# A three-phase attention and mixture-of-experts kernel: storage shared between the phases, the second phase's first group prepared in the tail of the first, and another order inside its steps

## The chip, the cores and the metric

The kernel runs on one core of one Trainium2 chip. The metric is the device time of one execution in microseconds (us). The kernel before took 5142.19 us, the median of three runs (5132.47 to 5145.69). One further execution was taken by the hardware profiler; all rows below are from that one.

## The reference

The input is x, 8 x 1024 tokens of 256 numbers, in float32. Three things are computed in turn.

**Phase A**, an attention over channels. For each token, 16 heads of 64 channels; within a head, each channel of q looks at the channels of k up to its own:

```python
Q = (x @ Wq + bq).reshape(b, s, H, C) * inv_sqrt_c
scores = jnp.einsum('bshq,bshk->bshqk', Q, K)        # C x C per token and head, causal mask
attn = jnp.einsum('bshqk,bshk->bshq', softmax(scores), V)
x = layernorm(x + attn.reshape(b, s, HID) @ Wo + bo)
```

**Phase B**, an attention over the first axis (8 rows) with 4 heads of 64, apart for each of the 1024 positions, with a residual and a norm:

```python
o = attention_over_rows(x @ in_proj_w.T + in_proj_b)   # L = 8, N = 1024
y1 = ln(x + o @ out_proj_w.T + out_proj_b) * ln1_g + ln1_b
```

**Phase C**, a mixture of 8 experts. A softmax of `y1 @ wg` picks one expert for each token; each expert takes at most 1024 tokens in order; an expert is two matrices with nothing between them (256 to 1024 to 256, with biases). The result times the gate is added to y1 and normed, x is added, and a last norm gives the output.

## The kernel before

PE (TensorE) multiplies, ACT (ScalarE) does exponentials and copies, DVE (VectorE) does everything elementwise, POOL (GpSimd) a few elementwise operations and the issuing of many small transfers; SP only issues transfers. Every engine takes its instructions in the order in which the program emits them, since all three phases stand in a manual schedule. Transfers of SP and ACT share eight completion slots each in turn, so an issue also waits for the transfer that had its slot before.

**Phase A** (`phase_a`) goes over 64 tiles of 128 tokens, t = 0 to 63, and one more turn of the loop, t = 64, for the tail. A tile has 8 steps c. In a step, `scores` is called three times (which = 2, 0, 1): it spreads k over block-diagonal operands L and q over R, and PE fills pairs of PSUM banks (`pair`, three of them); ACT takes the exponential `e`. `sums` multiplies `e` with the spread values V into one PSUM bank, `S` is DVE's copy of it (L395), and POOL moves S into `nd` by transfers. `divide` (L414) makes `att`, `turn` transposes it, `output` multiplies with Wo (L445), `normal` (L456) makes x1, and `store` writes x1 to DRAM (L418). R and L are filled by transfers in `build`, two buffers each: R on POOL's queue, L on SP's with 16 issues for each of the four rounds of a tile. `gather` sets an event on POOL (L316) after a round's transfers, and PE waits for that event. The tables `between`, `after`, `fill_a` and `fill_b` say which piece of the tile before or after is emitted in which step.

When phase A ends its pools are released. What phase B needs is then allocated in their place: weights, biases and constants are loaded or built, ahead of phase B's work.

**Phase B** (`phase_b`) goes over 8 groups j of 128 positions times 8 rows; group j takes tiles j, j + 8, ..., j + 56 of phase A. `load_x` reads them back from DRAM, `turn_x` transposes them (L662), `project_qk` (L677) and `project_v` (L695) project. A group has four steps n, one for each pair of heads and half of the positions. In a step, `scores` (L715, L726) fills `sc`, DVE takes the maximum mx (L735), ACT the eight exponentials s (L744), and `normed` divides by the sums (L754, L755). One step later `turn_s` transposes s into the same PSUM banks (L760), ACT copies that to sT (L762), and `weighted` multiplies with the values (L772); ACT copies it to oT (L780). `fills` lists for each group the other pieces, four lists: projections of the next group (`nxt`), `residual`, `output` (L802), `normal` (L816, L819), `exps` and `choice` of the group before (`prv`), and pieces of experts 0 and 1. `some(k)` emits the next k pieces of the list; what is left follows at the step's end. `fill` PSUM banks are three. The group j = -1 only prepares group 0: it calls `center` and `beside`, which fold the norm's gain into the router's weights, and projects group 0.

The order inside a step is this, in `phase_b`:

```python
st = scores(j, c, ib)
some(1)
weights(st, 0)
sT = turn_s(before[3])      # the step before
some(2 if live else 0)
weights(st, 1)
normed(st)
weighted(*before[:3], sT)
some(len(work))
```

**Phase C** (`phase_c`) ranks the tokens with small matrix products, builds one-hot matrices (L1032, L1183, L1185, L1195) to find each slot's token, then gathers the rows with POOL (L1218) and multiplies with each expert's product of matrices. `load` fetches experts 2, 3 and 4 when the phase starts (L1044), and `expert` multiplies the two matrices (L1063); ACT copies the product (L1072).

Of the kernel before, what the change touches and what calls it, by code (L numbers as in the profile page):

```python
# [24 lines left out]
FP = mybir.dt.float32  # L25
# [18 lines left out]
CAP = L * N // E  # L44
RW = 2 * D + 1
# [5 lines left out]
def fused_kernel(ctx: ExitStack, tc: tile.TileContext, a: dict, out: bass.AP):  # L51
# [28 lines left out]
    phase_a(tc, a, ident, x1_d, norm_scalars)  # L80
# [12 lines left out]
    phase_b(tc, a, ident, x1_d, rows_d, lg_d, keep, norm_scalars)  # L93
    phase_c(tc, a, ident, rows_d, keep, out)
# [27 lines left out]
def phase_a(tc, a, ident, x1_d, norm_scalars):  # L122
# [11 lines left out]
    with (  # L134
# [19 lines left out]
        for n in ("k", "q", "v"):  # L154
            w[n] = wp.tile([P, DC, HID], FP, name=f"w{n}")
            nc.sync.dma_start(w[n], a[f"W{n}"].rearrange("(c p) f -> p c f", p=P))
        for n in ("k", "q"):
            bias[n] = wp.tile([P, HID], FP, name=f"b{n}")
            nc.scalar.dma_start(bias[n], a[f"b{n}"].partition_broadcast(P))
# [38 lines left out]
        for i in range(2):  # L198
            Ls.append(wp.tile([P, 16, 4, 32], FP, name=f"L{i}"))
            R = wp.tile([P, 4, 8, C1], FP, name=f"R{i}")  # L200
            nc.gpsimd.memset(R, 0.0)
            Rs.append(R)
            V = wp.tile([P, 2, H1, 4, 32], FP, name=f"V{i}")
            nc.gpsimd.memset(V, 0.0)
            for aa in range(4):
                nc.gpsimd.memset(V[32 * aa : 32 * aa + 32, :, :, :, 8 * aa + 4 : 8 * aa + 5], 1.0)
            Vs.append(V)
# [252 lines left out]


# [47 lines left out]
        for t in range(NT + 1):  # L509
            live, more = t < NT, t + 1 < NT  # L510
            for c in range(8):
# [15 lines left out]
                for job in fill_a.get(c, ()):  # L527
                    side(t, job)
                if live:
                    scores(t, c, 0)  # L530
# [9 lines left out]
        store(NT - 1)  # L540


def phase_b(tc, a, ident, x1_d, rows_d, lg_d, keep, norm_scalars):
# [8 lines left out]
    with (  # L552
        tc.tile_pool(name="bw", bufs=1) as wp,
        tc.tile_pool(name="bgroup", bufs=2) as gp,
        tc.tile_pool(name="bx", bufs=3) as xp,
# [6 lines left out]
        wi = wp.tile([P, DC, 3 * D + E], FP, name="wi")  # L562
        nc.scalar.dma_start(wi[:, :, : 3 * D], a["in_wT"].rearrange("(c p) f -> p c f", p=P))
        bqk = wp.tile([P, 4], FP, name="bqk")
        nc.scalar.dma_start(bqk, a["in_b_qk"].rearrange("(c p) -> p c", p=P))
        nc.vector.tensor_scalar(bqk[:, 0:2], bqk[:, 0:2], HW**-0.5, None, ALU.mult)
        rows = {}
        for n in ("in_b_v", "out_b", "ln1_g", "ln1_b", "ln2_b"):
            rows[n] = wp.tile([P, D + E], FP, name=f"row_{n}")
            nc.scalar.dma_start(rows[n][:, :D], a[n].partition_broadcast(P))  # L570

# [4 lines left out]
        cols = {}  # L578
        for n in ("ln1_g", "ln1_b", "out_b"):
            cols[n] = wp.tile([P, DC], FP, name=f"col_{n}")  # L580
            nc.scalar.dma_start(cols[n], a[n].rearrange("(c p) -> p c", p=P), allow_slow_non_contiguous=True)
        wg = wp.tile([P, DC, E], FP, name="wg")
        nc.sync.dma_start(wg, a["wg"].rearrange("(c p) e -> p c e", p=P))
# [7 lines left out]

        rep = wp.tile([P, L, B], BF, name="rep")
        other = wp.tile([P, L, B], BF, name="other")
        nc.vector.memset(rep, 0.0)
        nc.vector.memset(other, 0.0)
        for h in range(2):
            r = slice(h * HW, h * HW + B)
            nc.vector.tensor_copy(rep[r], ident[r, None, r].to_broadcast([B, L, B]))
            nc.vector.tensor_scalar(other[r], rep[r], -1.0, MASKED, ALU.add, ALU.mult)

        G = {}
# [4 lines left out]

        ww = wp.tile([P, DC, 3, E], FP, name="ww")
        wrow = wp.tile([P, 2, E], FP, name="wrow")

        def column(n):  # L610
            return cols[n][:, :, None].to_broadcast([P, DC, E])

        def center():
            w = ww[:, :, 0, :]
            nc.vector.tensor_tensor(w, wg, column("ln1_g"), ALU.mult)
            ps = pf.tile([P, 512], FP, name="fill")
            for c in range(DC):
                nc.tensor.matmul(ps[:, :E], keep["ones"], w[:, c, :], start=c == 0, stop=c == DC - 1)
            mean = wp.tile([P, E], FP, name="mean")
            nc.vector.tensor_scalar(mean, ps[:, :E], 1.0 / D, None, ALU.mult)  # L620
            nc.vector.tensor_tensor(w, w, mean[:, None, :].to_broadcast([P, DC, E]), ALU.subtract)
            nc.vector.tensor_copy(wi[:, :, 3 * D :], w)
            nc.vector.tensor_tensor(ww[:, :, 1, :], w, column("out_b"), ALU.mult)
            nc.vector.tensor_tensor(ww[:, :, 2, :], wg, column("ln1_b"), ALU.mult)

        def beside():
# [10 lines left out]
            sums = ps[:, DC * E : (DC + 2) * E]  # L637
            for c in range(DC):
                nc.tensor.matmul(
                    sums,  # L640
                    keep["ones"],
                    ww[:, c, 1:, :].rearrange("p k e -> p (k e)"),
                    start=c == 0,
                    stop=c == DC - 1,
                )
            nc.vector.tensor_copy(wout[:, :, D:], ps[:, : DC * E].rearrange("p (k e) -> p k e", k=DC))
            nc.vector.tensor_copy(wrow, sums.rearrange("p (k e) -> p k e", k=2))
            nc.vector.tensor_copy(rows["in_b_v"][:, D:], wrow[:, 0, :])

        def load_x(j):  # L650
            G["x", j] = xp.tile([P, L, D], FP, name="x")
            nc.sync.dma_start(G["x", j], x1_v[j])

        def turn_x(j, l0):
            if l0 == 0:
                G["xT", j] = wp.tile([P, DC, NB, L, B], FP, name="xT")
                G["qk", j] = gp.tile([P, DC, 2, N], FP, name="qk")
# [30 lines left out]
        def project_v(j, b):  # L688

            xT = G["xT", j].rearrange("p c b l n -> p c b (l n)")  # L690
            if b == 0:
                G["v", j] = gp.tile([P, NB, D + E], FP, name="v")
# [6 lines left out]
            if b == NB - 1:  # L699

                for l in range(L):
                    nc.sync.dma_start(
                        lg_d[j].rearrange("(b n) l e -> l n b e", n=B)[l],
                        G["v", j][l * B : (l + 1) * B, :, D:],
                    )
                lg = xp.tile([P, L, E], FP, name="lg")
                nc.sync.dma_start(lg, lg_d[j])
                G["lg", j] = lg
# [190 lines left out]
        def fills(j):  # L899
# [13 lines left out]
            put(0, j < 0, center)  # L913
# [4 lines left out]
            put(0, j < 0, beside)  # L918
# [47 lines left out]
        for j in range(-1, NJ + 1):  # L966
            if j < 0:
                load_x(0)
                load_x(1)
            parts = fills(j)  # L970
            for n in range(4):
# [9 lines left out]
                live = 0 <= j < NJ  # L981
                if live:
# [5 lines left out]
                    st = scores(j, c, ib)  # L988
                    some(1)
                    weights(st, 0)  # L990
                if before:
                    sT = turn_s(before[3])
                    some(2 if live else 0)
                if live:
                    weights(st, 1)
                    normed(st)
                if before:
                    weighted(*before[:3], sT)
                before = None
# [7 lines left out]
def phase_c(tc, a, ident, rows_d, keep, out):  # L1007
# [6 lines left out]
    with (  # L1014
# [4 lines left out]
        tc.tile_pool(name="cexp", bufs=3) as xp,  # L1019
# [14 lines left out]
        ex = {}  # L1034
# [3 lines left out]
        def load(e, halves=(0, 1), behind=None):  # L1038
            if 0 in halves:
                ex[e] = [xp.tile([P, FC, D], FP, name=n) for n in ("w1", "w2")]  # L1040
# [41 lines left out]

        for e in range(EARLY, EARLY + 3):
            load(e)
# [343 lines left out]
```

## Time and profile before

| what | value |
| --- | --- |
| median of three runs | 5142.19 us |
| the profiled execution, its own time | 5148.31 us |
| its span, from the first to the last instruction | 5146.6 us |
| ACT busy | 3349.6 us, 65% |
| POOL busy | 3292.1 us, 64% |
| first scores of phase B (L715), group 0 | 4385.08 us |
| first scores of groups 1 to 7 | 4431.95, 4488.43, 4545.69, 4603.06, 4661.01, 4719.00, 4774.92 us |
| last group's tail (group index 8) begins | 4832.60 us |
| phase C's first product (L1088) | 4859.74 us |

The profile page lists the busy time of each engine over the span, the span in 40 slices, the transfer queues, the chain of work that ended last, and groups of instructions by line. In the rows that follow, a line such as L772 is a line of the kernel, `fill<-sT,v` is output and inputs by name, and a bracket holds how long the engine stood idle before and what released it. A busy engine isn't always the one that sets the end: what matters is what the others wait for in that stretch. So the profile is read by stretches.

### The profile page before, as it was taken

The page shows a single profiled execution, that of the slowest core. Times are in us where ns is not written, and L with a number is a line of the kernel's source. Part 1 is how long each engine was busy: PE and PEld are TensorE (multiplying, and loading weights), DVE is VectorE, ACT ScalarE, POOL GpSimd, SP SyncE. Part 2 cuts the span into 40 slices and gives each one's busy share as a digit, 9 for nine tenths or more (in the row PEclk, how much of TensorE's full clock was granted, in tenths as well). Part 3 has the DMA queues.
Part 4 walks back from the last instruction along what each step waited for, and adds up shares of the span by engine and source line. Part 5 has one row for each costly group of instructions (what it writes and reads, how often), then busy time and mean ns, then how long its engine had stood idle before and what let it go on. Part 6 is the DMA issues. An engine that isn't in the chain of part 4 may idle for free.

```text
span 5146.6 us, 189171 instructions
## 1 busy us (share of the span) xinstructions
PE 4878.0 (95%) x79320; PEld 3271.6 (64%) x79320; DVE 3118.9 (61%) x6241; ACT 3349.6 (65%) x4123; POOL 3292.1 (64%) x6950
## 2 busy tenths in 40 slices
PE   7999999999999999999999999999999997888674
PEld 4666666666666666666666666666666664555452
DVE  5666565666666666566566666666656563577756
ACT  4777777777777777777777777777777774444233
POOL 5767677677677676766766766776776774133245
PEclk9999999999999999999999999999999998999797
DMA  2222222222222222222222222222222222222442
GB/s 75 47 48 48 48 49 46 48 48 48 46 48 49 46 48 49 47 48 48 47 47 48 49 46 48 49 46 48 49 48 48 49 48 60 53 74 74 119 150 91
DMA packets 586955, 287.05 MB, mean 56 GB/s; under 512 B 406257, under 2 KB 537713, under 8 KB 586097
## 3 DMA queue, kind: packets, MB, share of 16 engines
q1 hardware_dynamic: 376802, 112.30, 11.1%
q0 software_dynamic: 204800, 159.82, 10.5%
q8 instruction: 620, 10.16, 0.9%
q10 hardware_dynamic: 4496, 2.83, 0.2%
q14 instruction: 237, 1.94, 0.1%
HBM read 72.84 MB, written 33.85 MB: 21 GB/s over the span
## 4 chain that ended last, share of the span: by engine, by line
PE 87%; DVE 6%; ACT 3%; DMA 2%; issue 1%; another core or an unknown queue 1%; POOL 0%; SPq 0%; ACTq 0%; DVEq 0%; POOLq 0%
PE pair L345 26%; PE sum L375 20%; PE sum L384 9%; PE pair L333 8%; PE ps L236 5%; PE ps L268 5%; PE ps L225 5%; PE ps L445 5%; PE ps L427 1%; PE fill L677 1%; ACT s L744 1%; DVE mx L735 1%; DMA w<-in_w 1%; PE fill L772 1%
## 5 line engine op out<-in xcount | busy, mean ns | idle before, releaser
L361 ACT ACTIVATE e<-pair 128x1024 f32<-128x1024 f32 x3072 | 2977.2, 1021 | 1237.9 <-PE pair L345 1237.9
L405 POOL DMA_DIRECT2D nd<-S x4096 | 1949.0, 484 | 608.3 <-DVE S L395 415.9
L345 PE MATMUL pair<-R,L 32*128 32x128 f32 (+1 forms) x32768 | 1606.5, 323 | 3.4 <-POOL event L316 3.4
L395 DVE COPY S<-sum 128x512 f32<-128x512 f32 x1024 | 707.1, 691 | 1468.1 <-PE sum L384 1147.0
L345 PEld LDWEIGHTS pair<-R,L 32*128 32x128 f32 x32768 | 1271.7, 186 | 49.8 <-POOL event L316 4.3
L375 PE MATMUL sum<-e,V 128*32 128x256 f32 x16384 | 1284.9, 385 | 4.9 <-DVE S L395 4.9
L302 POOL DMA_DIRECT2D R<-qm x2048 | 973.9, 483 | 74.4 <-issue 39.3
L384 PE MATMUL sum<-e,V 128*32 128x128 f32 x16384 | 823.3, 273 | 0.0
L384 PEld LDWEIGHTS sum<-e,V 128*32 128x32 f32 x16384 | 532.9, 110 | 352.2 <-issue 0.9
L375 PEld LDWEIGHTS sum<-e,V 128*32 128x32 f32 x16384 | 406.3, 109 | 236.6 <-DVE vT L243 41.8
L333 PE MATMUL pair<-late,sel 32*128 32x256 bf16 (+1 forms) x6144 | 499.3, 313 | 9.6 <-ACT e L361 9.6
L256 DVE COPY V<-vT 32x128 f32<-32x128 f32 x2048 | 457.2, 223 | 28.1
L414 DVE RECIPROCAL att<-nd 128x256 f32<-128x256 f32 x256 | 447.4, 1748 | 7.8 <-DMA nd<-S 3.9
L333 PEld LDWEIGHTS <-sel 32*128 32x128 bf16 x6144 | 155.4, 91 | 460.4 <-issue 445.0
L316 POOL MEMSET event<- 1x1 f32 x256 | 22.6, 88 | 622.2 <-DMA R<-qm 422.1
L225 PE MATMUL ps<-wk,xT 128*128 128x512 f32 x512 | 257.9, 627 | 10.9 <-DMA wk<-in_Wk 10.1
L236 PEld LDWEIGHTS ps<-xT,wv 128*128 128x128 f32 x2048 | 238.2, 191 | 44.4 <-issue 41.8
L236 PE MATMUL ps<-xT,wv 128*128 128x128 f32 x2048 | 262.6, 281 | 1.6 <-DVE qm L269 0.8
L268 PE MATMUL ps<-wq,xT 128*128 128x512 f32 x512 | 255.7, 622 | 6.4 <-DVE k L226 6.4
L74 POOL TENSOR_SCALAR ve<-mv 128x1 f32<-128x1 f32 x128 | 33.7, 263 | 356.4 <-DVE mv L72 354.2
L445 PE MATMUL ps<-wo,attT 128*128 128x256 f32 x1024 | 257.9, 395 | 0.7 <-ACT attT L428 0.7
L445 PEld LDWEIGHTS ps<-wo,attT 128*128 128x128 f32 x1024 | 186.1, 191 | 63.7 <-issue 41.8
(203 smaller groups left out, 3762.2 us busy)
## 6 DMA issues: line engine op xcount, KB each, us to landing
R<-qm POOLq DMA_DIRECT2D x2048, 32.0 KB
nd<-S POOLq DMA_DIRECT2D x4096, 16.0 KB
L<-k SPq DMA_DIRECT2D x4088, 8.0 KB
rows_d<-yx SPq DMA_DIRECT2D x32, 512.0 KB
xT<-in_xT SPq DMA_DIRECT2D x64, 128.0 KB
xr<-in_x SPq DMA_DIRECT2D x64, 128.0 KB
x_d<-x1o SPq DMA_DIRECT2D x64, 128.0 KB
x<-x_d SPq DMA_DIRECT2D x8, 1024.0 KB
```

The costliest lines, as they stand in the source:

```text
L225: nc.tensor.matmul(ps, xT_of[t][:, c, :], w["k"][:, c, cols], start=c == 0, stop=c == DC - 1)
L236: nc.tensor.matmul(ps[:, i * P : (i + 1) * P], w["v"][:, c, ch * P : (ch + 1) * P], xT_of[t][:, c, :], start=c == 0, stop=c == DC - 1,)
L268: nc.tensor.matmul(ps, xT_of[t][:, c, :], w["q"][:, c, cols], start=c == 0, stop=c == DC - 1)
L302: moved.append((None, nc.gpsimd.dma_start(R[:, b, s, b, :], q[:, b, s, cols])))
L333: nc.tensor.matmul(bank[u].rearrange("p (n i) -> p n i", i=n)[:, :, 0:32], sel[pr].rearrange("p a j -> p (a j)"), late[pr, None, :].to_bro ...
L345: one = nc.tensor.matmul(bank[u][:, x * 4 * n : (x + 1) * 4 * n].rearrange("p (b i) -> p b i", i=n), Lt[pr, 2 * (h0 + h) + jb].rearrange(" ...
L361: nc.scalar.activation(e, pair[i], AF.Exp)
L375: nc.tensor.matmul(dst[32 * u : 32 * u + 32], Vs[ww][:, 0, h0 + h, u, :], e0[u // 2][:, u % 2, x * 256 : (x + 1) * 256].rearrange("p (b i) ...
L384: nc.tensor.matmul(dst[32 * u : 32 * u + 32, :, 32:], Vs[ww][:, 1, h0 + h, u, :], e1[u // 2][:, u % 2, h * 128 : (h + 1) * 128].rearrange( ...
L395: nc.vector.tensor_copy(S[:, :, 2 * which : 2 * which + 2, :].rearrange("p b h i -> p h b i"), ps.rearrange("p (h b i) -> p h b i", h=2, b=4),
L405: nc.gpsimd.dma_start(tok[:, b, s, h0 * C1 : (h0 + G) * C1], Sx[:, 4 if s else b, b, :])
L445: nc.tensor.matmul(ps[:, :D], attT[:, c, :], wo[:, c, :], start=c == 0, stop=c == HID // P - 1)
```

## The change

The kernel's pool `both`, which lives through all phases, now holds the weights, biases, one R and one V of phase A, and small tiles of phase B. `view` gives names to parts of them for later: phase B's weights wi, its x, xT, qk and v buffers, and the storage of phase C's experts.

```diff
+    view = {
+        "wi": share["wk"][:, :, : 3 * D + E],
+        "x": [ share["wq"]..., share["R"]... ],
+        "xT": share["wv"]...,
+        "qk": share["V"]...,
+        "v": share["bias"]...,
+    }
+    view["experts"] = [
+        [matrix(share["wk"], "c f"), matrix(share["wq"], "c f")],
+        [matrix(share["wv"], "c f"), matrix(share["bias"], "k f")[:, :FC, :]],
+        [V[:, :FC, :], V[:, FC:, :]],
+    ]
```

The preparation of group 0, which was the group j = -1 of phase B, becomes functions of phase A with a table of when each is called, by tile and step; (NT, 8) comes after the last store.

```diff
+        lead = {
+            (NT - 1, 1): [(lead_load, 0)],
+            (NT - 1, 3): [(lead_load, 1), (lead_mask,)],
+            (NT - 1, 5): [(lead_logits,)],
+            (NT - 1, 6): [(lead_load, 2)],
+            (NT, 0): [(lead_turn, 0), (lead_turn, 1)],
+            (NT, 1): [(lead_qk, 0, 0)],
+            (NT, 2): [(lead_qk, 0, 1)],
+            (NT, 8): [
+                (lead_v, 0), (lead_v, 1), (lead_qk, 1, 0),
+                (lead_qk, 1, 1), (lead_v, 2), (lead_v, 3),
+            ],
+        }
...
                 for job in fill_a.get(c, ()):
                     side(t, job)
+                for fn, *args in lead.get((t, c), ()):
+                    fn(*args)
                 if live:
                     scores(t, c, 0)
...
         store(NT - 1)
+        for fn, *args in lead[NT, 8]:
+            fn(*args)
```

`lead_load(0)` issues seven transfers on SP, which were on ACT's and SP's queues after phase A: three columns (1 KB each), the router weights wg, wi (768 KB), bqk and the row in_b_v. `lead_load(1)` and `lead_load(2)` read x of groups 0 and 1 (1 MB each) from DRAM. `lead_mask` builds the two mask operands of the scores on DVE and scales bqk. `lead_logits` does what `center` did and half of `beside`:

```diff
+            ones = share["wk"][:, 0, HID - P :]
+            nc.vector.memset(ones, 1.0)
+            nc.vector.tensor_tensor(w, wg, column("ln1_g"), ALU.mult)
+            ps = pq.tile([P, 2, 512], FP, name="pair")
+            for c in range(DC):
+                nc.tensor.matmul(ps[:, 0, :E], ones, w[:, c, :], start=c == 0, stop=c == DC - 1)
+            nc.vector.tensor_scalar(mean, ps[:, 0, :E], 1.0 / D, None, ALU.mult)
...
+            for c in range(DC):
+                nc.tensor.matmul(ps[:, 1, : 2 * E], ones, ww[:, c, 1:, :]..., ...)
+            nc.vector.tensor_copy(wrow, ...)
+            nc.vector.tensor_copy(share["in_b_v"][:, D:], wrow[:, 0, :])
```

`lead_turn(k)` transposes four rows of x (8 PE transposes) with two copies each on DVE and ACT. `lead_qk` projects all 1024 columns of one q or k chunk into a `pair` and copies with one ACT instruction of 1024; `lead_v(k)` projects two of the eight blocks of v and adds the bias with one DVE instruction.

In phase B the loop begins at j = 0; `beside` keeps its other half as a piece of group 0, and the logits of group 0 are moved there too (`move_logits`). The tile `lg` has two buffers instead of three; x, qk and v have as many as before, some of them now in the views. The step is put in another order:

```diff
-                    st = scores(j, c, ib)
-                    some(1)
-                    weights(st, 0)
                 if before:
                     sT = turn_s(before[3])
-                    some(2 if live else 0)
                 if live:
+                    st = scores(j, c, ib)
+                    weights(st, 0)
+                    some(1)
                     weights(st, 1)
-                    normed(st)
+                    some(1)
                 if before:
                     weighted(*before[:3], sT)
-                before = None
+                    before = None
+                if live:
+                    some(1)
+                    normed(st)
                 some(len(work))
```

The loads of experts 2, 4 and 3 (2 MB each) move from the start of phase C into groups 7 and 8 of phase B, each at the head of a step:

```diff
+                e = {(NJ - 1, 1): EARLY, (NJ - 1, 2): EARLY + 2, (NJ, 0): EARLY + 1}.get((j, n))
+                if e is not None:
+                    for w, name in zip(view["experts"][e % 3], ("w1T", "w2")):
+                        nc.sync.dma_start(w, a[name][e].rearrange("(c p) d -> p c d", p=P))
...
-        for e in range(EARLY, EARLY + 3):
-            load(e)
```

## The prediction

> **What bounds the kernel now.** I read the page first: TensorE (PE) is busy 95% of the span, so time can only come from places where it is not. A table of stretches finds them. Columns: stretch, its length, busy time of PE, weight loads, DVE, ACT, POOL, then the granted PE clock, DMA share and GB/s.
>
> ```profile
> PE 4878.0 (95%) x79320; PEld 3271.6 (64%) x79320; DVE 3118.9 (61%) x6241; ACT 3349.6 (65%) x4123; POOL 3292.1 (64%) x6950
> ```
>
> ```profile
> 4316.00:4336.00 20.00, 10.56 (x65) 7.02 (x56) 8.30 (x10) 2.00 (x3) 4.34 (x9) 0.66 0.05 15
> 4336.00:4345.00 9.00, 0.00 (x0) 0.00 (x0) 1.45 (x4) 0.00 (x0) 4.34 (x20) 0.65 0.74 191
> 4345.00:4385.00 40.00, 30.06 (x96) 19.53 (x96) 7.87 (x28) 6.30 (x11) 2.51 (x2) 0.74 0.26 68
> 4506.00:4562.00 56.00, 46.74 (x284) 30.61 (x282) 41.21 (x97) 23.86 (x85) 17.41 (x24) 0.97 0.32 77
> 4868.00:4884.00 16.00, 10.45 (x36) 8.57 (x37) 12.17 (x35) 0.99 (x2) 0.00 (x0) 0.69 0.99 312
> ```
>
> Phase A, to about 4316, is a full PE: the change cannot shorten it. Between 4336 and 4345 PE does nothing, and up to 4385 it only prepares group 0 of phase B. The first phase-B scores (L715) start at 4385.08. What stands on that seam is in the chain of waits, in order of time:
>
> ```profile
> 4339.66 4.28 DMA acc<-in_b
> 4344.01 2.85 DMA x_d<-x1o
> 4346.90 8.06 DMA x<-x_d
> 4355.01 1.97 PE fill L662 x8
> ```
>
> The read of x waits behind the last store of x1. But group 0 takes tiles 0, 8, ... 56, which were stored long before.
>
> In phase B (4385 to 4860) I ask what PE waited for; columns are who waited for whom, us in total, times, longest:
>
> ```profile
> PE fill L772 <- ACT sT L762: 54.7, 31, 3.4
> PE fill L677 <- ACT xT L666: 14.1, 7, 5.0
> PE pw L876 <- DMA w<-in_w: 7.0, 1, 7.0
> ```
>
> The product with the values (L772) waits in all 31 steps for the copy of the transposed weights. One step's PE rows show why, and what follows:
>
> ```profile
> 4533.46 1.04 PE L760 MATMUL sc<-ident,s 128*128 128x128 f32 x8
> 4534.34 1.88 PE L677 MATMUL fill<-xT,wi 128*128 128x512 f32 x4
> 4539.39 1.30 PE L772 MATMUL fill<-sT,v 128*64 128x128 f32 x16 [3.17 <-ACT sT L762]
> 4540.62 5.14 PE L677 MATMUL fill<-xT,wi 128*128 128x512 f32 x8
> ```
>
> The transposes end at 4534.5, yet L772 starts at 4539.39: on ACT the copy stands behind four exponentials, which wait for DVE's maximum. The two projections after the wait take 5.14 us; 1.72 us each is their warm pace.
>
> **Part 1, the seam.** Seven loads, the two x loads, the masks, the centring of the router weights, the turns of x and all projections of group 0 move into the last tile and its tail.
>
> What it adds to tile 63, which is PE-bound:
> - lead_load(0) puts seven DMAs on SP between the L copies of rounds 1 and 2. Now round 2's last L is issued at 4276.3 and its event falls at 4282.29, while PE needs it at 4283.6. Seven issues at 0.5 us are 3.5 us, and the L copies behind them reuse the same eight completion slots, so each waits for a lead load. The small column loads and the 768 KB of weights take some 8 us from issue (col_out_b: 4347.4 issued, used 4355.9). The L copies then end near 4285.5: PE waits 3 us (0 to 8).
> - x(0), 1 MB in 8.06 us, stands ahead of round 3's L copies: they end near 4301 instead of 4295, needed at 4299.8 plus the 3 us: 0 (to 4).
> - lead_mask: seven DVE instructions of 0.11 to 0.22 us, and a wait for bqk. S copies stand behind it and PE behind them: 1 us (0 to 2).
> - lead_logits is a chain DVE, PE, DVE, PE inside PE's order. Rows L615 to L639 price it: four DVE pieces of 0.2 us on each side of two PE pieces of 0.5 to 1.0 us; with the S copy ahead (0.69) PE stands about 4 us (3 to 5).
> Together +8 us, all on the path.
>
> In the tail PE has holes. After the last sums (4318.6) come 16 transposes (2.2 us), copies until 4323.3, two full qk projections (3.44 us each warm, about 1 us more for cold): to 4331. The last division ends at 4327.9 as now, so turning att starts 3 us later, but the output product then runs at its warm 3.84 us instead of 6.67 and ends at 4336.8, against 4336.0. Then eight v (0.89 us each) and two qk, 14.0 us: 4350.8. Cover for the early part is the nd transfers; without it the two qk would cost 7 us. Add the 8 us of tile 63: first scores at 4359 against 4385.08. **Gain 26 us** (15 to 33). Late next is the tile-63 store, since the exponentials' buffers reuse its memory: 4346.9 plus 9 is 4356, before the first exponential near 4361.
>
> **Part 2, the step of phase B.** Transposes and the copy of sT now lead the step; scores and two fills stand between copy and product. From 0.9 (transposes) to 2.1 us (scores) the copy (1.02 us) is nearly through, so the 54.7 us vanish. The division (0.2 and 1.25 us) goes behind the product and a third fill; its reader is the next step's head. What can be late there: in the fourth step scores end 2.1 us in, maximum 1.4, eight exponentials 2.8, division 1.45, with the expert logits (1.1) beside: 8 us, while PE's work in that step is 9.3 us. That is the smallest slack; it closes if DVE is over 1.3 us behind.
>
> PE's work per group, start to start: scores 4 x 1.21, transposes 4 x 0.89, products 4 x 1.02, qk 8 x 1.72, v 8 x 0.94, outputs 8 x 0.94, turns of x 4 x 0.55: 43.5 us. The L715 rows put groups 1 to 6 at 4431.95 to 4774.92: 57.2 us each. What stays: in the first step the turns need ACT copies behind the exponentials, and outputs need the oT copy, 3.8 us (now 2.6 + 0.6 + 1.5); in the third step four yx instructions keep DVE from emptying a fill buffer, 1.2 us; clock after these gaps, 1 us. New group 49.5 us: 7.7 x 6 = **46 us**. Group 0 has no outputs (46.9 now, 41 after): 6 us. Group 7 (57.7 us, PE work about 34.5, DVE 38.6 of 50) loses its sT waits (about 9 us) but DVE stays late: 7 us.
>
> Two rules bear on this. The Trainium skill, page "TensorE: Matmul & The Clock Gate", section "Why this matters for your kernels", says that PE gaps of over some 3 us halve its clock. Taken as a threshold, only the waits near 3.2 and 3.4 us would give back clock beyond their length: one a group, 1.6 us x 7 = 11 us on top of 54.7. The table shows PE 46.74 busy against 43.5 of warm work at granted clocks of 0.91 to 0.97: 3.2 us a group. I take the row. Against the change speaks "SBUF — State Buffer", section "Who interferes with whom": DVE with two SBUF inputs and GpSimd exclude each other for a whole instruction. In the trace yx takes 0.48 us alone and 1.44 beside POOL, on average 0.76. If squeezing the same POOL work (17.4 us a group) into 49 us collides in proportion, 16 x 0.28 us of delay grows by a sixth, 0.7 us a group; were all 16 to collide, 11 us and the gain were gone. I take the first; it is hidden while DVE's 41.2 stays below 49.5.
>
> **Part 3, phase C.** Experts 2, 4 and 3 are loaded during groups 7 and 8, into storage that is free by then. Now 6 MB start at 4867.98; expert 2's product ends at 4883 and ACT's one-hot work queues behind its copy, so DVE stands 4.46 us for buffers. That goes: **4.5 us** (0 to 10). The 2 MB pieces (16 us for 6 MB now, so 5 us each) sit on SP behind or ahead of the small expert pieces by one step: nothing. The logits tile has two buffers instead of three, so its load waits on SP for the choice of the older group; behind it stand gate rows, which need that choice anyway: nothing. Storage itself costs nothing in phase A: its instructions and waits keep their order until tile 63.
>
> **Sum.** 26 + 46 + 6 + 7 + 4.5 = 89.5 us. The profiled execution took 5148.31 us (span 5146.6, 1.7 around it): 5058.8. The median of the runs, 5142.19, lies 6.1 lower: **5053 us**.
>
> **Rivals.**
> - DVE becomes the bound. For: 41.2 of 56 us are busy, and it works in order between PE results; in groups the maximum often starts late. Against: it sat idle before many rows of the fourth step. A group of 52.5 us gives 28 instead of 46, group 7 nothing, one us less at the seam: 63 us, 5079 us.
> - PE reaches its work: groups of 45 us (73), seam 32, group 0 and 7 together 18, phase C 7: 130 us, 5012 us. For: only ACT copies stand against it.
> - Slower: the head transposes stand in PE's order for the division. The gains, 89.5 us over 31 steps, are gone once each head waits 2.9 us. At 4 us it is 31 x 4 = 124 us on top of 5053: 5177 us. For: DVE lags 2 us into the fourth step (maximum at 4764.63, scores done at 4762.6). Against: slack of 1.3 us and more in all steps, and the fills behind the division.
> - The loads starve tile 63: round 2 and 3 each late by 10 us instead of 3: seam gains 9, 5070 us.
> - It does not do what it says, x(0) still waiting for the last store: excluded by the built instruction order, where that load waits for an older DMA slot alone; under 1%.
>
> **Chances.** Forecast 0.52, DVE bound 0.25, PE bound 0.12, starved 0.06, slower 0.05. What a measurement of this kernel can tell from none is about 0.3%, 15 us; only the slower case and a sliver of DVE's lie there: faster 0.93, same 0.02, slower 0.05. Range 5012 to 5098: from the PE case to DVE-bound groups of 55 us with 21 us at the seam (44.7 us in all).
>
> **What would show it.** First scores near 4359, with a PE stop of some 4 us at the two small products in tile 63 and 3 us at an event before it; group starts 49 to 50 us apart; no wait of L772's successor for sT; few waits of the transposes for DVE; ACT's one-hot work about 7 us earlier behind expert 2. I am wrong if the transposes wait for s by over a microsecond a step, or if fills wait mostly for DVE.

## The result, and the profile after

The changed kernel took 5108.86 us, the median of five runs (5100.91 to 5113.82), beside 5142.19 us (5132.47 to 5146.78) before: a ratio of 0.9931, 95% interval 0.992 to 0.9943. It is faster by 33 us where 89 were forecast, below even the smallest gain in the range. The profiled executions differ by 39.8 us in span (5146.6 and 5106.8), and that difference divides as follows; each row is the difference of two start times in the two traces.

| stretch | forecast gain | measured gain |
| --- | --- | --- |
| seam, to the first scores (4385.08 and 4365.44) | 26 | 19.6 |
| group 0 | 6 | 2.6 |
| groups 1 to 6, start to start | 46 | 11.0 |
| group 7 to the last `hot` (4859.3 and 4820.9) | 7 | 5.2 |
| phase C, from there to the end | 4.5 | 1.4 |

The last row can't be read as a gain or as none: two traces of the changed kernel, on two chips, differ there by 9.2 us (285.9 and 276.7).

The page's engine row says that PE is busy for 13 us less in a span 40 us shorter, so most of what was gained is idle time, as meant.

```profile
PE 4865.3 (95%) x79320; PEld 3262.3 (64%) x79320; DVE 3119.7 (61%) x6238; ACT 3351.0 (66%) x4119; POOL 3299.0 (65%) x6950
```

The table of stretches of the changed kernel (columns as before) shows that the seam has been filled: no stretch without PE is left, and the clock is up. The last row is a group of phase B, 55.6 us long, and PE is busy in it for 46.78 us.

```profile
4329.00:4349.00 20.00, 15.40 (x82) 9.08 (x83) 9.63 (x14) 5.01 (x9) 3.90 (x8) 0.91 0.05 14
4349.00:4365.44 16.44, 15.64 (x57) 10.24 (x56) 4.09 (x8) 2.23 (x2) 6.85 (x22) 1.00 0.39 100
4519.35:4574.95 55.60, 46.78 (x281) 31.29 (x281) 41.98 (x96) 24.23 (x85) 18.45 (x24) 0.97 0.32 77
```

What PE waited for in groups 0 to 6, first in the kernel before (4385.08 to 4775 us), then in the changed one (4365.44 to 4742 us); columns: who for whom, us in total, times, longest.

```profile
PE fill L772 <- ACT sT L762: 45.9, 27, 3.3
```

```profile
PE fill L934 <- ACT oT L912: 28.6, 6, 5.6
PE fill L807 <- ACT wv L796: 9.4, 7, 1.5
PE fill L934 <- DVE lg L939: 5.6, 6, 1.1
```

The wait for sT went, all 45.9 us of it. A new one took 28.6 back, the output's (L934, formerly L802) for oT: 3.0 us in group 1 and 4.8 to 5.6 in each of groups 2 to 6. With the small ones all waits listed for these groups came down only from 61.4 to 52.2 us, and 45.8 of these 52.2 are waits for ACT.

The steps of a group, from the start of one step's scores to the next (medians of groups 2 to 5), show where. Step 3 gained what was hoped, step 0 lost most of it.

| | step 0 | step 1 | step 2 | step 3 |
| --- | --- | --- | --- | --- |
| before | 16.5 | 12.9 | 12.7 | 15.8 |
| after | 19.3 | 13.1 | 12.9 | 10.9 |
| the forecast's count | 15.6 | 12.2 | 12.5 | 9.2 |

The last row splits the forecast's 49.5 us by step, with the pieces that `fills` puts into each: PE work of 10.8, 12.2, 11.3 and 9.2 us; 3.8 us of waits and 1 us of clock in step 0; 1.2 us in step 2.

One step 0 in the timeline, engine by engine (start, us, instruction, and in brackets the idle time and its releaser). PE:

```profile
4576.18 1.09 PE L904 MATMUL fill<-sT,v 128*64 128x128 f32 x16
4577.20 1.09 PE L792 MATMUL fill<-ident,x 128*128 128x128 f32 x8
4583.49 2.13 PE L934 MATMUL fill<-wout,oT 128*128 128x264 f32 x4 [5.20 <-ACT oT L912]
```

The product L904 runs without a wait, as forecast, and is done at 4577.2; its copy oT is what the output needs. ACT:

```profile
4580.05 0.37 ACT L876 ACTIVATE s<-sc,mx 128x128 f32<-128x128 f32 x1 [3.93 <-DVE mx L868]
...
4582.81 0.63 ACT L912 COPY oT<-fill 128x512 f32<-128x512 f32 x1
4583.27 0.44 ACT L796 COPY wv<-fill 128x256 f32<-128x256 f32 x1
```

ACT stands 3.93 us for the maximum, then does eight exponentials, and only then the copy that PE has needed since 4577.2, and after that the copies of x. DVE says why the maximum is late:

```profile
4575.68 1.01 DVE L1027 SCALAR_TENSOR_TENSOR acc<-w,b,acc 128x256 f32<-128x256 f32 x2 [2.65 <-DMA w<-in_w]
...
4578.51 1.22 DVE L867 TENSOR_REDUCE mx<-sc 128x8 f32<-128x1024 f32 x1
```

The scores were done near 4576.2. DVE had waited 2.65 us for a weight, a quarter of w2 (256 KB), the second matrix of an expert, which `expert_bias` needs in step 3; then it did the eight instructions of `choice`. The program issues that load at the head of step 3, behind 1 MB of x on SP:

```profile
4567.34 0.42 SPq L782 DMA_DIRECT2D x<-x_d  x1
4567.81 1.07 SPq L996 DMA_DIRECT2D w<-in_w  x1
```

SP had stood at two transfers of yx, which wait for DVE's `normal`, and came to these two only then. Issued at 4567.81, the weight was used at 4575.68. In the kernel before it took as long (issued 4592.16, used 4599.82) with a wait of 0.82. Step 3 has become 5 us shorter, its load has not. DVE's waits for it over the groups, before and after (4366 to 4800 us in both):

```profile
DVE acc L895 <- DMA w<-in_w: 5.1, 5, 1.9
DVE acc L1027 <- DMA w<-in_w: 13.0, 5, 3.1
```

The five waits after stand at the starts of groups 2 to 6, which took 54.5 to 57.1 us. Group 1 has none and took 52.6 us.

### The profile page after: what moved, and what is told of

Same layout as the page of the kernel before. It is cut to its first block, busy times and chain, and to the rows that moved or that the text cites. A ratio compares the mean times of both kernels' runs of the same rounds, so it can differ in the third digit from the quotient of the medians.

```text
span 5106.8 us, 189156 instructions
## 1 busy us (share of the span) xinstructions
PE 4865.3 (95%) x79320; PEld 3262.3 (64%) x79320; DVE 3119.7 (61%) x6238; ACT 3351.0 (66%) x4119; POOL 3299.0 (65%) x6950
## 5 line engine op out<-in xcount | busy, mean ns | idle before, releaser
L389 PEld LDWEIGHTS pair<-R,L 32*128 32x128 f32 x32768 | 1272.3, 186 | 54.5 <-POOL event L360 8.8
L269 PE MATMUL ps<-wk,xT 128*128 128x512 f32 x512 | 257.5, 626 | 11.8 <-DMA wk<-in_Wk 11.1
L76 POOL TENSOR_SCALAR ve<-mv 128x1 f32<-128x1 f32 x128 | 33.9, 265 | 305.8 <-DVE mv L74 286.8
```

Source lines behind the costliest of these rows:

```text
L389: one = nc.tensor.matmul(bank[u][:, x * 4 * n : (x + 1) * 4 * n].rearrange("p (b i) -> p b i", i=n), Lt[pr, 2 * (h0 + h) + jb].rearrange(" ...
```

## The experiments

Each kernel is the changed one with one edit or several, timed against the kernel before on the same chip. Three chips were used, and the kernel before took 5098.67, 5140.77 and 5147.96 us on them; so ratios are compared, not times. The chips differ mostly in phase C: from the last `hot` to the end it takes 243 to 244 us in the traces of the first chip and 277 to 293 in all others. "Groups" is the time from the start of group 1 to that of group 7 in each trace, "step 0" the mean of groups 2 to 5.

| kernel | ratio (95%) | groups | step 0 |
| --- | --- | --- | --- |
| before | 1 | 343.0 | 16.6 |
| changed | 0.9931 (0.992 to 0.9943) | 332.0 | 19.4 |
| changed, again | 0.9927 (0.9913 to 0.994) | 331.8 | 19.3 |
| old order everywhere | 0.9956 (0.9942 to 0.9969) | 337.8 | 16.7 |
| old order in step 0 | 0.9937 (0.9923 to 0.995) | 334.0 | 20.8 |
| w2 earlier | 0.9906 (0.989 to 0.9921) | 320.2 | 17.2 |
| last output first | 0.9931 (0.9918 to 0.9945) | 339.0 | 21.2 |
| w2 earlier, old order in step 0 | 0.9906 (0.989 to 0.9921) | 319.6 | 17.6 |
| w2 earlier, last output first | 0.9896 (0.9881 to 0.9911) | 318.7 | 16.2 |
| the same, turns ahead | 0.9872 (0.9857 to 0.9887) | 312.9 | 15.4 |
| lead moved | 0.9905 (0.989 to 0.992) | 332.4 | 19.3 |
| turns ahead, lead moved | 0.9868 (0.9853 to 0.9883) | 315.6 | 16.1 |
| expert loads late | 0.9943 (0.9929 to 0.9956) | 330.5 | 19.3 |
| division at once | 0.9947 (0.9933 to 0.996) | 338.7 | 19.1 |

The changed kernel itself was run twice, to see how much of a ratio is the chip's.

> The changed kernel once more, unaltered, as the standard on the chip of these runs. If chips differ only in the part that is outside this change, its ratio to the kernel before is 0.993 again and its first scores of the second phase start at 4364 to 4366 us.

The ratio agrees; the first scores came at 4361.17, 4 us earlier than in the first trace. That much is phase A's own: counted from one fixed instruction of tile 62 (a product with Wo, at 4238.05 in the first trace) the two agree to 0.3 us, 127.4 and 127.1 us.

**What the order of the step is worth.** Two kernels put the old order back, in every step or in step 0 alone:

```diff
-                if before:
-                    sT = turn_s(before[3])
                 if live:
                     st = scores(j, c, ib)
+                    some(1)
                     weights(st, 0)
-                    some(1)
-                    weights(st, 1)
-                    some(1)
+                if before:
+                    sT = turn_s(before[3])
+                    some(2 if live else 0)
+                if live:
+                    weights(st, 1)
+                    normed(st)
                 if before:
                     weighted(*before[:3], sT)
...
-                if live:
-                    some(1)
-                    normed(st)
```

> Keeps the shared storage, the seam and the early expert loads; takes the order inside every step of the second phase back to that of the kernel before. Theory 1 (step 0 of a group pays for the new order, step 3 gains by it): step 0 back to about 16.5 us, steps 1 and 2 near 12.8, step 3 near 14.5 to 15.5, groups near 56.5 to 57.5 us, so about 10 to 15 us slower than the changed kernel, 5118 to 5124 us; still about 20 to 25 us faster than the kernel before, by the seam and the loads alone. Rival A (VectorE is the bound of a group whatever the order): the time stays within 5 us of the changed kernel. Rival B (the new order is a loss on the whole): faster than the changed kernel.

> The old order in step 0 of each group only, the new one in steps 1 to 3. Theory 1: step 0 back from 19.5 to about 16.5 us, step 3 stays at about 11, so seven groups give back about 3 us each: 15 to 21 us faster than the changed kernel, 5088 to 5094 us. Rival A (VectorE is the bound): what step 0 gives back step 1 loses, within 5 us of the changed kernel. Rival B (step 0 is long for its transposes and loads, not for its order): step 0 stays above 18.5 us.

The first came out as theory 1 had it: 0.9956 against 0.9927 to 0.9931, groups 5.8 us longer in all, group 0 3.2. So the new order is worth 12 us by the trace (first scores to last `hot`), 13 to 15 by the ratios, and the seam and the loads the rest. The second was a miss. Step 0 did not fall to 16.5, it rose to 20.8, as rival B had it, and the ratio did not move beyond its interval. So the order of step 0 alone was not what made it long. In its waits (PE, 4300 to 4850 us) the wait for sT is back in step 0, where PE stands in place of oT:

```profile
PE fill L904 <- ACT sT L894: 33.0, 8, 5.8
```

**The late weight.** The load of the last quarter of w2 is issued ahead of x:

```diff
-                    if j < E - EARLY:
+                    if j < E - EARLY and n < 3:
                         load_expert(EARLY + j, n, False)
...
+                if n == 2 and j < E - EARLY:
+                    load_expert(EARLY + j, 3, False)
                 if n == 2 and 0 <= j and j + 2 < NJ:
                     load_x(j + 2)
```

> The w2 load of the last quarter is issued at the end of step 2, ahead of the next group's x instead of behind it. Theory 1: VectorE's wait of 2.6 us for in_w ahead of the first weighted sum of step 0 goes, and with it the choice and the exponentials come 2 to 2.5 us earlier in six groups: 10 to 14 us faster than the changed kernel, 5095 to 5099 us. Rival A (VectorE is the bound): more, if anything, since its idle time is all that is left to gain, 15 us. Rival C (the wait only hides another that ends as late): less than 4 us.

The groups became 11.8 us shorter, and the ratio fell by 0.0021 to 0.0025, 11 to 13 us: theory 1's 10 to 14. Rival C is out; the 15 us of rival A lie within the uncertainty of this number. DVE's wait for in_w is gone from the trace (13.0 us in five waits before the edit). Group 1, which had not waited for the load, stayed as it was (52.6 and 52.5 us); groups 2 to 6 became 2.3 us shorter on average. Step 0 still waits 3.0 us for oT in each of seven groups, 21.1 in all.

**The output ahead of the exponentials.**

```diff
+                if before and n == 0:
+                    weighted(*before[:3], sT)
+                    before = None
                 if live:
                     weights(st, 0)
```

> In step 0 of each group the turn of the last output (its product and its copy oT) is issued straight after the scores, ahead of the exponentials, so that ScalarE copies oT before them. Theory 1: the 4.6 us for which TensorE waits for oT in each of seven groups goes and the clock stays up after it: 22 to 32 us faster than the changed kernel, 5077 to 5087 us, step 0 at 14.5 to 16 us. Rival A (VectorE is the bound): the choice, the sums and the products of VectorE stay as late as they are, step 1 gets longer by what step 0 gives up, within 6 us of the changed kernel.

This refuted theory 1. The wait for oT went, and the ratio stayed at 0.9931; step 0 even rose to 21.2 and the groups by 7.0 us. Rival A had the number right, but not the place: step 1 kept its 13.1 us. PE's waits of this kernel (4300 to 4850 us):

```profile
PE fill L792 <- ACT wv L796: 23.3, 8, 4.8
```

The turns of x now wait for their own copies on ACT, behind the same exponentials. Hence a second theory: in step 0 ACT is one line of copies and exponentials whose start is the maximum; whichever item PE needs first, it waits. The late w2 delays the start, the place in the line decides the rest. Two kernels test it, each with the early w2.

> The old order in step 0 and the early w2 together. Theory 2 (what made step 0 long is the late w2, whatever the order): step 0 falls from 20 to 21 us to 16.5 to 17.5, seven groups to about 54 us, 10 to 18 us faster than the old order in step 0 alone and within 6 us of the early w2 alone. Rival (the old order itself makes step 0 long, by the wait for sT behind the exponentials): step 0 stays above 18.5 us.

> Both edits of step 0 at once: the w2 load of the last quarter ahead of x, and the turn of the last output ahead of the exponentials. Theory 2 (ScalarE in step 0 is a single line of sT, oT, eight exponentials and the copies of x, and it starts when the maximum comes; the late w2 only delays that start): the wait for oT (3.0 us a group with the early w2) goes and the transposes of x wait 1.5 to 3 us for their copies instead, step 0 at 16 to 17 us, within 8 us of the kernel with the early w2 alone. Theory 1 (the wait for oT is itself the cost): 3 us in each of seven groups, 18 to 21 us faster than the early w2 alone, step 0 at 14.5 us or less.

With w2 in time the old order gives 17.6 us, a tenth above theory 2's span, and the new one 17.2, and the ratios are the same: theory 2. Output first brings 16.2 us and a ratio 0.001 lower than the early w2 alone, within its interval, with the turns waiting 11.7 us in seven waits, also as theory 2 had it. So the order inside step 0 hardly mattered, and the same move that cost 7.0 us in the groups beside a late w2 gained 1.5 with it in time.

Then the copies of x were put at the head of the line too, behind oT and ahead of the exponentials:

```diff
                     weighted(*before[:3], sT)
                     before = None
+                    some(4 if j + 1 < NJ else 2)
```

> On top of the early w2 and the early last output: in step 0 the first two turns of x are also issued ahead of the exponentials, so that their copies stand before them on ScalarE. Theory 2 (ScalarE's line in step 0 is what TensorE waits for): the 11.7 us for which the second turn waits for a copy go to under 3, step 0 from about 16.3 to 15 us, 6 to 12 us faster than that kernel, ratio near 0.988. Rival (VectorE's half of the copies, behind the maximum, is as late as ScalarE's): within 4 us of it.

Ratio 0.9872, step 0 at 15.4 us, groups 5.8 us shorter, at the lower edge of what theory 2 gave. (The ratio fell by 12 us, but in the two traces 3.5 us of it lie at the seam, which this edit doesn't touch.) The waits (PE, 4359 to 4850 us) show that most of it moved one place on: the first projection of q, which had waited 8.4 us for the last copy of x, now waits 21.1. All waits of PE for copies of x fell only from 29.7 to 23.4 us.

```profile
PE fill L807 <- ACT wv L796: 21.1, 7, 3.3
PE fill L792 <- ACT wv L796: 2.3, 2, 1.7
```

That wait is 3.30 us in each of groups 1 to 6, and still step 0 takes 13.9 us in one of them and 16.8 in another. The granted clock (the last but two of each row) tells them apart, and the same four products behind the same wait:

```profile
4506.57:4520.44 13.87, 10.57 (x79) 8.21 (x78) 11.24 (x31) 6.47 (x23) 3.70 (x6) 1.00 0.19 34
4557.28:4574.04 16.76, 13.46 (x79) 9.60 (x78) 12.03 (x31) 6.46 (x23) 4.09 (x7) 0.80 0.32 66
```

```profile
4515.88 1.99 PE L807 MATMUL fill<-wv,wk 128*128 128x512 f32 x4 [3.30 <-ACT wv L796]
4566.57 3.78 PE L807 MATMUL fill<-wv,wk 128*128 128x512 f32 x4 [3.30 <-ACT wv L796]
```

So a difference of under 1 us between two kernels' steps 0 can be the clock's alone.

**The lead in the last tile.**

```diff
-            (NT - 1, 1): [(lead_load, 0)],
-            (NT - 1, 3): [(lead_load, 1), (lead_mask,)],
-            (NT - 1, 5): [(lead_logits,)],
+            (NT - 1, 5): [(lead_load, 0), (lead_load, 1)],
             (NT - 1, 6): [(lead_load, 2)],
-            (NT, 0): [(lead_turn, 0), (lead_turn, 1)],
+            (NT, 0): [(lead_mask,), (lead_turn, 0), (lead_turn, 1)],
...
+            (NT, 3): [(lead_logits,)],
```

> The seam's small loads, both x loads, the masks and the router's two small products leave the rounds of the last tile: the loads go to the end of that tile's rounds, the products behind the first projections in the tail. Theory: the 5.7 us of event waits and the 2.2 us of waits at the two small products go, and the products after them run at full clock: last sums at about 4319 to 4321 us instead of 4329.6. The tail then waits for the loads or for the last products instead: first scores 4 to 10 us earlier, 4355 to 4361 us. Rival (the tail is bound by its own loads and the last store, tile 63 is hidden): first scores within 2 us of 4365.

First scores at 4357.26; counted from the same fixed instruction as above, 9.4 us earlier than in the changed kernel on the same chip. The median is 6.5 us below. So tile 63 paid for the lead as the prediction had said, and paid more. In the changed kernel's timeline, PE in tile 63 and the tail:

```profile
4300.71 0.61 PE L547 MATMUL pair<-ww,wk 128*128 128x8 f32 x4 [1.31 <-DVE ww L544]
4302.16 1.04 PE L554 MATMUL pair<-ww,wk 128*128 128x16 f32 x4 [0.84 <-DVE ww L552]
...
4303.31 1.92 PE L389 MATMUL pair<-R,L 32*128 32x256 f32 x16
...
4329.57 0.64 PE L419 MATMUL sum<-e,V 128*32 128x256 f32 x8 [0.90 <-DVE S L439]
...
4335.08 8.83 PE L584 MATMUL pair<-wv,wk 128*128 128x512 f32 x16 [2.10 <-ACT wv L573]
```

Two short waits, and then products at half pace (1.92 us instead of 1.04). PE's waits for POOL's event in the rounds of this tile are 5.7 us, against 2.3 with the lead moved and 2.0 in the kernel before.

Both places together:

> The last one with the seam's loads and small products moved out of the last tile's rounds as well. The two places are independent, so the gains add: 6 to 7 us faster than the kernel without the seam's edit, ratio 0.986 to 0.988 to the kernel before, faster than both kernels. If the loads of the tail collide with the second phase's first group the gain at the seam is lost again and the two are within 3 us.

Its ratio, 0.9868, is the lowest of the study, 0.6% below that of the changed kernel, but the one without the seam's edit is the same within the intervals, and its median is even 1.6 us lower: the gains did not add. From the fixed instruction to the first scores this kernel takes 122.3 us, and the one without the seam's edit 122.9, where the ten other traces with the lead in tile 63 have 126.2 to 128.5. So the kernel it is compared with had gained some 4 us at the seam with no edit there. And in this kernel's own tail a part of the edit's gain was lost:

```profile
4317.98 1.96 PE L569 MATMUL pair<-ident,wq 128*128 128x128 f32 x16
4323.14 8.83 PE L584 MATMUL pair<-wv,wk 128*128 128x512 f32 x16 [3.21 <-ACT wv L573]
...
4336.73 6.04 PE L489 MATMUL ps<-wo,attT 128*128 128x256 f32 x16 [0.68 <-ACT attT L472]
```

In the kernel with the lead alone moved the same rows took 7.13 and 3.72:

```profile
4327.32 7.13 PE L584 MATMUL pair<-wv,wk 128*128 128x512 f32 x16 [3.20 <-ACT wv L573]
...
4338.75 3.72 PE L489 MATMUL ps<-wo,attT 128*128 128x256 f32 x16 [0.68 <-ACT attT L472]
```

Same order, same wait, 4 us apart by the clock. In the groups, too, it is slower than the kernel without the seam's edit, by 1.4 us in group 0 and 2.7 in groups 1 to 6, with the same waits of 3.3 us in step 0. Whether the loads of the tail collide with group 0, as the expectation feared, isn't shown.

**The two remaining parts.** The division straight behind the exponentials:

```diff
                     weights(st, 1)
+                    normed(st)
                     some(1)
...
                     some(1)
-                    normed(st)
```

> The division follows the exponentials at once in VectorE's order instead of behind the product and a third fill; all else is as in the changed kernel. Theory 2 (the step's end is set by TensorE's own work, the weights have slack of microseconds everywhere but in step 0): VectorE then stands 2 to 3 us for the last exponential while fills wait to be emptied, so 0 to 8 us slower than the changed kernel, and the early transposes do not wait for s either way. Rival (the deferral costs, since the next step's transposes wait for the division): faster than the changed kernel by 5 us or more.

0.9947, groups 6.7 to 6.9 us longer: at the upper end of theory 2's span or just over it, and the rival is out. DVE's waits of this kernel (4361 to 4800 us) carry 75.1 us for the exponentials' sums, against 45.4 in the changed kernel:

```profile
DVE sm L886 <- ACT s L876: 75.1, 32, 3.6
```

And the expert loads put back behind phase B:

```diff
-                e = {(NJ - 1, 1): EARLY, (NJ - 1, 2): EARLY + 2, (NJ, 0): EARLY + 1}.get((j, n))
-                if e is not None:
+                for e in (EARLY, EARLY + 2, EARLY + 1) if (j, n) == (NJ, 3) else ():
```

> The loads of experts 2, 4 and 3 go to the end of the last step before the third phase, all three at once, behind the second phase's own transfers; all else is as in the changed kernel. Forecast's term (the early loads are worth 4.5 us): 4 to 5 us slower than the changed kernel, ratio to before near 0.994, VectorE idle for expert 2's buffers again. Rival (whatever they gain the third phase loses again at a later wait, as the profile of the changed kernel suggests with 1.4 us): within 3 us of the changed kernel's 0.993.

0.9943, 0.0012 to 0.0016 above the changed kernel, 6 to 8 us with an uncertainty of about as much. That fits 4.5 us and doesn't shut out the rival. In its trace DVE idles 11.2 us at one place for the load of an expert, and phase C takes 293.1 us from the last `hot` to the end. The three other traces of that chip, with the loads early, have 279.8, 285.3 and 286.8: all shorter, but 7 us apart among themselves.

## Why the prediction was wrong

**Where it held.** The waits for sT vanished as forecast, and no wait of the head transposes for the division is listed in groups 0 to 6 of the changed kernel, so the slower rival is out. Step 3 went from 15.8 to 10.9 us, the largest gain of the change. Of the two signs that would have shown it wrong, neither came: the transposes do not wait for s, and the fills wait mostly for ACT. It failed elsewhere: 35 of the 50 us that the trace misses of the forecast lie in groups 1 to 6.

**The step that failed** is the 3.8 us put down for step 0, "the turns need ACT copies behind the exponentials, and outputs need the oT copy", with 1 us for the clock. These waits were priced near what they had been, 4.7 us, and it was taken for granted that the maximum would still come straight after the scores. In the group shown, step 0 took 19.8 us where the count gave 15.6; these 4.2 us are the largest part of the 7.1 us by which that group missed 49.5.

```profile
4574.95:4594.75 19.80, 13.39 (x81) 10.11 (x82) 13.59 (x37) 6.48 (x23) 3.04 (x6) 0.83 0.15 22
```

Its waits are 5.20 and 1.22 us, 6.4 together, and PE is busy for 13.4 us at a granted clock of 0.83, where 10.8 of work and 1 for the clock were counted. The work itself was counted rightly: at a granted clock of 1.00 it took 10.57 us (the kernel with the turns ahead). With the w2 load issued earlier the waits of step 0 are 4.0 to 4.4 us in groups 2 to 5, near the forecast's 3.8, and the step falls from 19.4 to 17.2 us. So the late load is the cause of the longer wait. With oT and the turns at the head of ACT's line the step falls by another 1.8 us, to 15.4, but only 0.8 of that are waits; the best kernel, with the same order and waits, has 16.1. That 15.4 lies so near the forecast's 15.6 is in part luck with the clock.

The prediction looked at the 2 MB loads of phase C beside "the small expert pieces" and called them nothing. It never asked when a small piece must land once its step is a third shorter; its wait was in the trace before, 0.82 us in this group.

**The PE work of 43.5 us a group** was the second mis-sized term. The prediction saw 46.74 us busy and put the 3.2 us between down to a cold clock. The table of stretches of the kernel with w2 earlier, steps 1 to 3 of one group:

```profile
4531.66:4544.76 13.10, 12.98 (x77) 8.56 (x78) 9.55 (x23) 5.67 (x20) 5.13 (x8) 1.00 0.36 94
4544.76:4557.66 12.90, 11.81 (x73) 7.86 (x74) 12.05 (x26) 5.67 (x20) 8.43 (x10) 1.00 0.21 62
4557.66:4568.46 10.80, 9.74 (x59) 5.57 (x60) 8.54 (x20) 6.39 (x22) 1.81 (x2) 1.00 0.65 173
```

The clock is granted in full, and net of the listed waits (none, 1.08 and 1.06 us) these steps take 13.1, 11.8 and 9.7 us against 12.2, 11.3 and 9.2 in the count: 2.0 us a group that no clock and no listed wait accounts for, a tenth of a microsecond or two at many changes from one kind of product to the next. Group 1 of the changed kernel says the same: at a granted clock of 1.00 PE is busy in it for 45.7 us. A price from a row of one kind, back to back, was taken for work that alternates; that this is the cause is a guess that wasn't tried, and step 0, which alternates too, kept to its count at full clock. The last 1.0 us of the group's miss is a wait of the last projection in step 3 for ACT to empty a buffer, which was not in the count.

**The two rules.** For the clock the prediction took the row of its table, 3.2 us lost in a group, of which 1 would stay. Over groups 1 to 6 PE was busy for 48.4 us a group before and 47.2 after, so 1.2 us came back, less than the 2.2 of the row and the 1.6 of the threshold. DVE and POOL did not collide more: an instruction of DVE on yx took 0.76 us on average before and 0.72 after.

**The seam** gave 19.6 instead of 26. The mechanism was right, each place was where the prediction put it. Tile 63 lost 12 us, not 8: the sums that wait for the last S start at 4329.57 instead of 4317.13. Of these, 3.7 us are longer waits for POOL's event and 2.2 the waits at the two small products; the rest was not taken apart, but rows at half pace stand behind both. The two early projections took 8.83 us after a wait of 2.1 us, where 7.9 were put down for them, 6.9 and 1 for cold.

**Group 0, group 7 and phase C** gave 9.2 instead of 17.5 us and were not taken apart further. Phase C's 4.5 us neither fell nor was shown.

**The rival that DVE becomes the bound** had groups of 52.5 us, nearer to the 55.3 measured than the forecast, but for another reason: DVE's busy time stayed at 42 us a group while order and a load alone brought the groups to 52.2 us (312.9 over six). DVE was late because it stood in order behind a load, not because it was full.

## What to carry to other kernels

A wait that is taken away shows its worth only after the next item in that engine's line has been priced: here 45.9 us of waits went and 28.6 came back one instruction further on, on the same engine. When a step gets shorter, list every load that is issued in it and must land in it, however small: its time from issue to landing does not shrink, and an in-order engine passes its lateness on to all that stands behind. And an edit that is judged beside an unmended wait can look worse than worthless: the output first cost 7.0 us in the groups alone and was part of the best version once w2 came in time. Before a microsecond between two kernels is given a cause, compare their listed waits and their granted clock: the same order with the same waits gave steps of 13.9 to 16.8 us.

## What the runs showed of the hardware

The length of a gap did not decide whether PE's pace was halved after it. In the kernel with the turns ahead the same four products stand behind the same wait of 3.30 us in six groups: they took 1.99 us in one group and 3.13 to 3.78 in the other five, and the granted clock of the step was 1.00, 0.89 or 0.80. In the tail, after a wait of 2.1 us in front of the same sixteen products, ten traces had them at 8.83 us and one, that with the turns ahead, at 7.13; after 3.20 us one had 7.13 and one 8.83. Behind the two small products of tile 63, after the same waits of 1.31 and 0.84 us, the next sixteen products took 1.92 us in eight traces and 1.04 in three.

The Trainium skill, page "TensorE: Matmul & The Clock Gate", section "What's actually happening", says that the clock gate judges activity in windows of 3.4 us that run freely. What a gap costs would then depend on where it falls in them, and these rows agree. They go against reading as a threshold the 3 us that the prediction cites from that page: 3.30 us once cost nothing, and 2.1 us mostly cost clock. In front of the 2.1 us stand sixteen transposes of 1.97 us, and no run here shows whether these count as activity.
